# A graph-attention kernel: ScalarE fetches a tile of edges by hand in every 16th pair instead of every 64th, applies z's slope first in its round, and SyncE's queue is reordered

## The chip, the cores and the metric

The kernel runs on one core of one Trainium2 chip. The metric is device time in microseconds (us), taken from runs without the profiler; one further run was profiled. The kernel before takes 3905.68 us (median of three runs, 3905.53 to 3908.12).

## The reference

One layer of a graph network over 12500 nodes with 128 features and 400000 directed edges, each edge with 32 features. The edges arrive sorted by destination; their sources are random.

```
h    = relu(layernorm(x))
n    = layernorm(h) * g1 + b1
x_l, x_r = n @ W_l, n @ W_r                        # 12500 x 128, as 8 heads x 16
e    = edge_attr @ W_e                             # 400000 x 128
m    = leaky_relu(x_l[src] + x_r[dst] + e, 0.2)
alpha = sum over c of m * att                      # one score for each edge and head
a    = softmax of alpha over the edges of one destination (and a loop edge for each node)
h    = h + segment_sum(x_l[src] * a, dst) + bias
out  = x + h + W2 @ gelu(W1 @ layernorm(h))        # written here without its biases
```

What matters here is `x_l[src]`: 400000 rows of 544 bytes (128 features and 8 ones) that lie scattered in a DRAM table, `xl_dram`, and have to be brought into on-chip memory 128 at a time.

## The kernel before, in words

The kernel has three stages. The **node stage** (lines 792 to 879) normalises the nodes and writes `xl_dram` and a part of `xr_dram`, while GpSimd (POOL) already gathers 116 tiles of raw node rows (`raw_gather`, L339), which serve 29 of the later pairs. The **edge stage** (`window_edges`) takes up nearly all the time. The **node groups** (`f_...` steps) finish 25 groups of four tiles of 128 nodes (three in the first and the last) while the edge stage goes on; the last two end it.

The edge stage works in 782 *pairs* of 512 edges, four *tiles* of 128 edges each. A round r of the loop at L1680 writes out, for each engine, one step of each of some ten pairs; every engine then runs its own list in that order, and semaphores alone tie the lists together. The steps of a pair c, with the engine, the round and the line:

- `gather` (POOL, round c-4, L1078): one indirect DMA for each tile of 128 rows, into `xs`, a ring of 12 pairs.
- `combine` (TensorE, round c, L1143 and L1146): turns the four tiles into the PSUM bank `z` and adds the edges' and destinations' part. `apart` (TensorE, round c+2, L1152).
- `slope` (ScalarE, round c+1, L1157): `zs` = 0.2 z. `bend` (VectorE, round c+1, L1162): `m` = max(z, zs).
- `score` (TensorE, round c+2, L1167), `lowest` (VectorE, round c+3, L1173): `rec`.
- `weigh` (ScalarE, round c+3, L1184): `p`, two exponentials. `turn` (TensorE, round c+4, L1192): `pt_ps`.
- `keep_turned` (ScalarE, round c+5, L1197): copies `pt_ps` to `pt`.
- `collect` (TensorE, round c+6, L1206), `own_heads` (VectorE, round c+7, L1215 and L1221).
- `put` (SyncE, round c+8, L1230): stores `rec` to the states in DRAM.

SyncE (SP) also starts the loads of four pairs at once (`windows`, L1104 to L1119), the clearing of states (`clear`, L787), the sums over edge features (`sum_load`, L1248, 98 loads in the first 196 rounds), and the loads and stores of the node groups.

Two ways go around POOL for single tiles. For 35 pairs (every 22nd from 30) SyncE fetches the fourth tile row by row, and for 11 pairs (every 64th from 77) ScalarE does: `hand` (L1037) starts, spread over the 22 or 64 rounds that end six rounds before the pair, 128 DMAs of one 544-byte row each (L1056), whose addresses it reads into registers sixteen at a time (L1010) from `hand_sb`. `gather` then leaves that tile out. One round before the pair, the fetching queue waits until all 128 rows have landed (L1043). `hand_sb` is filled in the node stage: two DMAs (L841) pick the indices out of `src` element by element, and VectorE scales them (L851).

In each round the loop runs `hand` for both ways after all steps on the engines, then `clear`, then `windows`, then `put`. A store carries no order against other stores where rows were fetched in its round (`if fetched`); in the last rounds, where none are, each store waits until the one before has landed.

The steps of the last but one node group stand in the table `soon`, by rounds counted from that group's round, 774: its exponential at +2 (`f_exp`), its square root at +7 (`f_root`), its scaling at +8 (`f_scale`).

Of the kernel before, what the change touches and what calls it, by code (L numbers as in the profile page):

```python
# [13 lines left out]
F32 = mybir.dt.float32  # L14
# [8 lines left out]
P = 128  # L23
# [52 lines left out]
BESIDE_EVERY = 64  # L76
BESIDE_FIRST = 77
BESIDE_LANDED = 3
BESIDE_AT = 64
BIG = 2.0**126  # L80
# [94 lines left out]
def tile_gnn(  # L175
# [112 lines left out]
    def load_consts():  # L288
        for i, v in enumerate((ln2_g, ln2_b, None, b1[0:P], b1[P : 2 * P])):
            if v is not None:  # L290
                nc.sync.dma_start(cols[:, 2 + i : 3 + i], column(v))
        nc.sync.dma_start(att_c, bass.AP(tensor=att.tensor, offset=att.offset, ap=[[1, C], [C, H], [1, 1]]))
        nc.sync.dma_start(we_sb, bass.AP(tensor=w_e.tensor, offset=w_e.offset, ap=[[P, DE], [0, QP], [1, P]]))
        nc.sync.dma_start(weh_sb[WN:P, :], w_e)
        nc.sync.dma_start(w1_sb, w1)
        nc.sync.dma_start(w2_sb, w2.rearrange("(k p) f -> p k f", p=P))
        nc.sync.dma_start(bias_r, row_bcast(bias, P))
        nc.sync.dma_start(b2_r, row_bcast(b2, P))
        nc.sync.dma_start(first_sb, bass.AP(tensor=dst.tensor, offset=dst.offset, ap=[[0, 1], [UP * U, NU // UP]]))
        for i in range(QP):  # L300
            nc.sync.dma_start(
                at_sb[:, BEHIND:, 1 + i],
                bass.AP(tensor=dst.tensor, offset=dst.offset + (UP * i + 1) * U, ap=[[0, 1], [QU * U, NQU]]),
            )

# [504 lines left out]
    with tc.manual_schedule():  # L810
# [15 lines left out]
        for r in range(max(max(len(qs), 9) + LAST + 1, 16 + PARTS, rows_at[-1] + KEPT + 1)):  # L826
# [11 lines left out]
            if r == 14:  # L838
                nc.sync.dma_start(src_sb, src)
                for at, h in ((0, hands), (BESIDE_AT, beside)):  # L840
                    nc.sync.dma_start(  # L841
                        hand_sb[at : at + len(h)],
                        bass.AP(
                            tensor=src.tensor, offset=src.offset + (h[0] + 1) * UP * KU - 1,
                            ap=[[h.step * UP * KU, len(h)], [NCH * K, P]],
                        ),
                    )
            if r == 16:
                for at, h in ((0, hands), (BESIDE_AT, beside)):
                    rows = hand_sb[at : at + len(h)]  # L850
                    nc.vector.tensor_scalar(rows, rows, float(XW * 4), None, op0=OP.mult)  # L851
# [101 lines left out]
def window_edges(  # L953
# [30 lines left out]
    with ExitStack() as es:  # L984
# [52 lines left out]
        def hand(r, w):  # L1037

            w["new"].clear()
            hands, n = w["pairs"], w["sems"]  # L1040
            i, k = divmod(r + HAND_LEAD + hands.step - hands[0], hands.step)
            if k == HAND_LEAD - 1 and 0 < i <= len(hands):
                all_here = w["queue"].wait_ge(w["landed"][(i - 1) % n], ((i - 1) // n + 1) * P * 16)  # L1043
                tc.declare_fence(all_here.ins, group=f"{w['name']}{i - 1}")
# [3 lines left out]
            if k == 0:  # L1048
                d["x"] = once.tile([P, XW], F32, name=f"{w['name']}{i % 2}")
            for e in range(P * k // hands.step, P * (k + 1) // hands.step):  # L1050
                if e % HAND_READ == 0:
                    d["at"] = words(
                        hand_sb[w["at"] + i : w["at"] + i + 1, e : min(e + HAND_READ, P)], (NT * P - 1) * XW * 4,
                        w["engine"],
                    )
                row = w["queue"].dma_start(  # L1056
                    d["x"][e : e + 1, :].bitcast(U8), rows_at(xl_dram, d["at"][e % HAND_READ], 1, XW * 4)
                )
# [166 lines left out]
        def put(c):  # L1225
# [11 lines left out]
            if fetched:  # L1237
# [3 lines left out]
                )  # L1241

# [3 lines left out]
        def sum_load(i):  # L1246
            sums[i] = fin.tile([P, LW], F32, name="ea_s", tag="big", bufs=3)
            nc.sync.dma_start(  # L1248
# [295 lines left out]
        def f_put(d):  # L1544
# [4 lines left out]
            (LATE + 1, own_heads),  # L1549
            (5, keep_turned),  # L1550
# [6 lines left out]
            (1, slope),  # L1557
# [3 lines left out]
        )  # L1561
        late_stages = (
            (-WAHEAD, windows),
            (LATE + PUT, put),
# [115 lines left out]
        with tc.manual_schedule():  # L1680
            for r in range(-AHEAD, max(last_round, groups[-1]["round"] + 18)):
                in_round(r, early, groups[:-2])
                for late, f in stages:
                    c = r - late
                    if 0 <= c < n_pr:
                        f(c)
                for late, f in sum_stages:
# [11 lines left out]
                for w in ways:  # L1699
                    hand(r, w)  # L1700
# [364 lines left out]
```

## Time and profile before

| | us |
|---|---|
| median of three runs | 3905.68 |
| the profiled execution's own time | 3904.92 |
| its span, first to last instruction | 3903.2 |
| POOL's first gather of the edge stage starts | 153.92 |
| POOL's last gather starts | 3854.66 |

A page of the profile gives busy times by engine and the costliest groups of instructions. In a row of a group stand the line, the engine, the operation, the output and inputs by the program's names, the count, then the busy time, the mean of one in ns, and the time that the engine sat idle just before these, with what ended that idle time ("issue": nothing that the profile shows). "ACTq" and "SPq" are the instructions with which ScalarE's and SyncE's sequencers start DMAs or load registers; they are not counted as busy.

### The profile page before, as it was taken

The numbers are of one execution on the slowest core, as the hardware profiler recorded it, in microseconds if no ns is written. First come the engines' busy times: TensorE is split into PE (matmuls) and PEld (weight loads), VectorE is DVE, ScalarE is ACT, GpSimd is POOL, SyncE is SP. The second block draws the span as 40 slices with busy tenths as digits, with TensorE's granted clock in tenths as the row PEclk, the third lists the DMA queues.
The fourth block names the chain that finished last, engine by engine and source line by source line (L and its number), as shares of the span: only waits on it lengthen the run. The fifth ranks groups of instructions, "written<-read, shape, count | busy, mean of one in ns | idle before, by whom it ended". The sixth has DMA issues, their size and how long they took to land.

```text
span 3903.2 us, 70516 instructions
## 1 busy us (share of the span) xinstructions
PE 3414.5 (87%) x18461; PEld 2329.9 (60%) x18463; DVE 2799.8 (72%) x6142; ACT 2177.5 (56%) x4745; POOL 2913.6 (75%) x3092
## 2 busy tenths in 40 slices
PE   3588899889899989998999899999998989898988
PEld 3356566556566666665666666666666666666655
DVE  5577877777776776777777777777777767667665
ACT  6545555555565555555555555655555556456444
POOL 7777777777777777777777777777777777777773
PEclk6799999999999999999999999999999999999999
DMA  8767777777766666665565555555565555555553
GB/s 203 236 163 173 184 184 182 177 185 185 177 135 134 136 131 130 137 132 125 123 131 124 123 126 126 125 123 121 121 125 126 123 123 112 124 122 117 122 119 65
DMA packets 546765, 549.30 MB, mean 141 GB/s; under 512 B 248891, under 2 KB 425372, under 8 KB 545932
## 3 DMA queue, kind: packets, MB, share of 16 engines
q1 hardware_dynamic: 444290, 329.68, 34.3%
q0 software_dynamic: 98528, 214.12, 28.9%
q8 instruction: 150, 2.46, 0.3%
q14 instruction: 261, 2.14, 0.2%
q10 hardware_dynamic: 3536, 0.91, 0.1%
HBM read 482.08 MB, written 62.28 MB: 139 GB/s over the span
## 4 chain that ended last, share of the span: by engine, by line
PE 36%; POOL 24%; DMA 20%; issue 13%; DVE 2%; SPq 1%; ACT 0%; ACTq 0%; POOLq 0%
POOL xs L1078 24%; DMA xs<-xl_dram,src_sb 19%; PE z L1146 8%; PE acc L1206 8%; PE ab L1167 6%; PE pt_ps L1192 4%; PE z L1143 4%; PE ab L1152 2%; PE acc L1525 1%; DMA state<-rec 0%; DVE rec L1173 0%; PE acc L1500 0%; PE pt_ps L759 0%; DMA zw<-xr_dram 0%; PE acc L1328 0%
## 5 line engine op out<-in xcount | busy, mean ns | idle before, releaser
L1078 POOL DMA_INDIRECT xs<-xl_dram,src_sb x2963 | 2798.4, 944 | 904.3 <-issue 783.9
L1184 ACT ACTIVATE p<-ab,rec 128x256 f32<-128x256 f32 x1563 | 656.4, 471 | 923.6 <-DVE rec L1173 909.3
L1215 DVE TENSOR_TENSOR own<-acc,diag 128x272 f32<-128x272 f32 x782 | 342.6, 438 | 821.9 <-PE acc L1206 813.2
L1143 PE MATMUL z<-ident,xs 128*128 128x128 f32 x3079 | 564.7, 283 | 360.6 <-DMA xs<-xl_dram,src_sb 337.9
L1206 PE MATMUL acc<-xs,pt 128*128 128x136 f32 x6158 | 873.7, 286 | 0.0
L1143 PEld LDWEIGHTS z<-ident,xs 128*128 128x128 f32 x3079 | 395.3, 142 | 776.8 <-DMA xs<-xl_dram,src_sb 449.7
L1146 PE MATMUL z<-ea,zw 128*128 128x512 f32 x1564 | 828.0, 612 | 6.5 <-DMA xs<-xl_dram,src_sb 6.5
L1197 ACT COPY pt<-pt_ps 128x512 f32<-128x512 f32 x782 | 456.2, 583 | 643.6 <-PE pt_ps L1192 585.5
L1167 PE MATMUL ab<-m,negrep 128*128 128x512 f32 x1564 | 806.4, 597 | 0.2 <-issue 0.2
L1206 PEld LDWEIGHTS acc<-xs,pt 128*128 128x128 f32 x6158 | 800.7, 197 | 0.0
L1192 PEld LDWEIGHTS pt_ps<-ident,p 128*128 128x128 f32 x3125 | 408.0, 146 | 345.0 <-issue 269.7
L1162 DVE TENSOR_TENSOR m<-z,zs 128x512 f32<-128x512 f32 x782 | 533.6, 682 | 108.1 <-ACT zs L1157 106.2
L1129 DVE TENSOR_SCALAR ea<-dl,wid 96x516 f32<-96x516 bf16 x782 | 575.4, 736 | 8.0 <-DMA dl<-dc_dram 8.0
L1173 DVE TENSOR_REDUCE rec<-ab 128x2 f32<-128x512 f32 x781 | 539.0, 690 | 14.2 <-PE ab L1167 13.7
L1192 PE MATMUL pt_ps<-ident,p 128*128 128x128 f32 x3125 | 490.7, 281 | 0.6 <-ACT p L1184 0.6
L1157 ACT ACTIVATE zs<-z 128x512 f32<-128x512 f32 x782 | 471.8, 603 | 31.0 <-PE z L1146 31.0
L1221 DVE TENSOR_REDUCE rec<-own 128x34 f32<-128x272 f32 x782 | 340.9, 436 | 26.7
L1152 PE MATMUL ab<-ne,farw 128*128 128x512 bf16 (+1 forms) x781 | 306.8, 393 | 24.6 <-ACT p L1184 22.9
L1146 PEld LDWEIGHTS z<-ea,zw 128*128 128x128 f32 x1564 | 253.1, 202 | 7.3 <-issue 6.8
L1167 PEld LDWEIGHTS ab<-m,negrep 128*128 128x128 f32 x1564 | 245.8, 195 | 1.1 <-DMA ea_s<-in_ea_t 0.7
L1152 PEld LDWEIGHTS <-farw 128*128 128x128 bf16 x782 | 78.1, 100 | 211.9 <-issue 102.2
L1184 ACT ACT_TABLE_LOAD x102 | 130.9, 1283 | 1.8
(249 smaller groups left out, 2215.6 us busy)
## 6 DMA issues: line engine op xcount, KB each, us to landing
dl<-dc_dram SPq DMA_DIRECT2D x196, 396.0 KB
hand<-xl_dram SPq DMA_DIRECT2D x4480, 0.5 KB
ea<-in_ea_t SPq DMA_DIRECT2D x196, 256.0 KB
ea_s<-in_ea_t SPq DMA_DIRECT2D x98, 512.0 KB
xs<-xl_dram,src_sb POOLq DMA_INDIRECT x2963
beside<-xl_dram ACTq DMA_DIRECT2D x1408, 0.5 KB
state<-empty SPq DMA_DIRECT2D x98, 144.0 KB
f_st<-state SPq DMA_DIRECT2D x46, 288.0 KB
```

The costliest lines, as they stand in the source:

```text
L1078: nc.gpsimd.indirect_dma_start(out=xs[:, j, :], out_offset=None, in_=xl_dram, in_offset=bass.IndirectOffsetOnAxis(ap=src_sb[:, c * KP + j ...
L1129: nc.vector.tensor_scalar(d["ea"][0:WN].rearrange("p (a b) -> p a b", b=OW), d["dl"][0:WN].rearrange("p (a b) -> p a b", b=OS)[:, :, 0:OW] ...
L1143: nc.tensor.matmul(z[:, j * P : (j + 1) * P], row_of(c, j)[:, 0:P], ident, start=(j == 0), stop=False, is_transpose=True)
L1146: nc.tensor.matmul(z[:, :e], d["zw"], d["ea"][:, :e], start=False, stop=True)
L1152: nc.tensor.matmul(d["ab"][:, :e], d["far"], d["ne"][:, :e], start=True, stop=False)
L1157: nc.scalar.activation(d["zs"][:, :e], d["z"][:, :e], AF.Copy, scale=SLOPE)
L1162: nc.vector.tensor_tensor(d["m"][:, :e], d["z"][:, :e], d["zs"][:, :e], op=OP.max)
L1167: nc.tensor.matmul(d["ab"][:, :e], negrep.rearrange("p n h -> p (n h)"), d["m"][:, :e], start=False, stop=True)
L1173: nc.vector.tensor_reduce(d["rec"][:, :, CX], d["ab"].rearrange("p (u e) -> p u e", e=U), AX.X, OP.min)
L1184: nc.scalar.activation(d["p"][:, us], d["ab"][:, us], AF.Exp, bias=d["rec"][:, i, CX:SH], scale=-1.0)
L1192: nc.tensor.transpose(d["pt_ps"][:, js], d["p"][:, js], ident)
L1206: nc.tensor.matmul(d["acc"][:, i, :], d["pt"][:, j * P : (j + 1) * P], row_of(c, j), start=(j == js[0]), stop=(j == js[-1]),)
```

## The change

1. The distance of the pairs whose fourth tile ScalarE fetches falls from 64 to 16, and the first is pair 29 instead of 77: 47 pairs instead of 11. POOL has 36 indirect DMAs fewer. ScalarE starts 47 x 128 = 6016 row DMAs instead of 1408 and loads registers from `hand_sb` 376 times instead of 88.
2. ScalarE's rows of a round no longer stand together at its end: half follow `keep_turned`, a quarter `weigh`, and a quarter `slope` of the next round. `slope` moves ahead of `keep_turned` and so is first in ScalarE's round.
3. `hand_sb` is no longer filled by DMA: in rounds 24 to 26 of the node stage VectorE copies the wanted columns of `src_sb` as floats, TensorE turns them, VectorE scales them.
4. SyncE's rows are split, half at the start of a round and half after the steps; then comes `put`, then `windows`, then `clear`. After each fourth store the registers for the next four pairs are loaded ahead.
5. The last three stores no longer wait for the landing of the one before (they wait for the last hand-fetched tile instead).
6. `sum_load`'s 98 loads go out on ScalarE's queue instead of SyncE's.
7. In `soon` the steps from `f_exp` on come 1 to 3 rounds earlier: square root at +4, scaling at +5.

```diff
-BESIDE_EVERY = 64
-BESIDE_FIRST = 77
+BESIDE_EVERY = 16
+BESIDE_FIRST = 29
...
+    def hand_columns():
+        nc.vector.memset(hand_f, 0.0)
+        for at, h in ((0, hands), (BESIDE_AT, beside)):
+            first = (h[0] + 1) * UP * KU - 1
+            step = h.step * UP * KU
+            nc.vector.tensor_copy(
+                hand_f[:, at : at + len(h)], src_sb[:, first : first + step * (len(h) - 1) + 1 : step]
+            )
+    def hand_turn():
+        hand_ps["t"] = once_ps.tile([P, GN * P], F32, name="w_ps")
+        nc.tensor.transpose(hand_ps["t"][0 : BESIDE_AT + len(beside), 0:P], hand_f, ident)
+    def hand_bytes():
+        nc.vector.tensor_scalar(
+            hand_sb, hand_ps["t"][0 : BESIDE_AT + len(beside), 0:P], float(XW * 4), None, op0=OP.mult
+        )
...
-                for at, h in ((0, hands), (BESIDE_AT, beside)):
-                    nc.sync.dma_start(
-                        hand_sb[at : at + len(h)],
...
-        def hand(r, w):
+        def hand(r, w, share=(0, 1), behind=0):
...
-            for e in range(P * k // hands.step, P * (k + 1) // hands.step):
+            first, last = P * k // hands.step, P * (k + 1) // hands.step
+            for e in range(*(first + int((last - first) * x) for x in share)):
...
+            free = bool(fetched) or c > hands[-1]
+            if free and not fetched:
+                nc.sync.wait_ge(ways[0]["landed"][(len(hands) - 1) % LANDED], ((len(hands) - 1) // LANDED + 1) * P * 16)
...
-            if fetched:
+            if free:
...
+            if c % QP == 0 and c + QP < n_pr:
+                ats(c // QP + BEHIND + 1)
...
-            nc.sync.dma_start(
+            nc.scalar.dma_start(
                 sums[i],
...
             (LATE + 1, own_heads),
+            (1, slope),
             (5, keep_turned),
...
-            (1, slope),
...
+        beside_at = {keep_turned: ((0, 0.5),), weigh: ((0.5, 0.75),), slope: ((0.75, 1), 1)}
         late_stages = (
+            (LATE + PUT, put),
             (-WAHEAD, windows),
-            (LATE + PUT, put),
...
-            (2, f_exp),
-            (3, f_den),
-            (4, f_out),
-            (5, f_h),
-            (6, f_stats),
-            (7, f_root),
-            (8, f_scale),
-            (8, f_rest),
+            (1, f_exp),
+            (2, f_den),
+            (2, f_out),
+            (3, f_h),
+            (3, f_stats),
+            (4, f_root),
+            (5, f_scale),
+            (5, f_rest),
...
+                hand(r, ways[0], (0, 0.5))
                 in_round(r, early, groups[:-2])
...
+                    if f in beside_at:
+                        hand(r, ways[1], *beside_at[f])
...
-                for w in ways:
-                    hand(r, w)
+                hand(r, ways[0], (0.5, 1))
+                for late, f in late_stages:
+                    c = r - late
+                    if 0 <= c < n_pr:
+                        f(c)
...
-                for late, f in late_stages:
-                    c = r - late
-                    if 0 <= c < n_pr:
-                        f(c)
```

Three places show what the engines' lists become. A row is a line of the program, the operation, output and input, the shape, and how many such stand in a row; `beside` is ScalarE's hand-fetched tile, `hand` SyncE's.

ScalarE in the middle of the edge stage, kernel before, one round (with one step for later nodes' `xr` rows, L669, such as stands in some rounds):

```order
L1197 COPY pt<-pt_ps 128x512
L1157 ACTIVATE zs<-z 128x512
L1184 ACTIVATE p<-ab,rec 128x256 x2
L669 ACTIVATE xr_14292<-pt_ps,cols 128x512
L1056 DMA beside_11620<-xl_dram 1x544 x2
```

The same engine in the changed kernel, one round:

```order
L1176 ACTIVATE zs<-z 128x512
L1075 DMA beside_24432<-xl_dram 1x544 x2
L1216 COPY pt<-pt_ps 128x512
L1026 TENSOR_LOAD hand_sb
L1075 DMA beside_24432<-xl_dram 1x544 x4
L1203 ACTIVATE p<-ab,rec 128x256 x2
L1075 DMA beside_24432<-xl_dram 1x544 x2
```

`zs` now comes ahead of `pt`; eight row DMAs a round stand in three places where two stood in one, and in every second round, as here, a register load stands between `pt` and `p`.

SyncE around the loads of four pairs, before:

```order
L787 DMA state<-empty 128x2x144
L1010 TENSOR_LOAD at_sb
L1104 DMA ea<-in_ea_t 32x4x512
L1109 DMA dl_1711<-dc_dram 96x2112
L1114 DMA du_1714<-du_dram 64x1x512
L1119 DMA zw_1705<-xr_dram 96x512
L1230 DMA state<-rec 96x2x72
L1056 DMA hand_23106<-xl_dram 1x544 x6
```

and in the changed kernel:

```order
L1252 DMA state<-rec 96x2x72
L1026 TENSOR_LOAD at_sb
L1123 DMA ea<-in_ea_t 32x4x512
L1128 DMA dl_1713<-dc_dram 96x2112
L1133 DMA du_1716<-du_dram 64x1x512
L1138 DMA zw_1708<-xr_dram 96x512
L809 DMA state<-empty 128x2x144
L1075 DMA hand_30322<-xl_dram 1x544 x6
```

The store has moved from behind the four loads to ahead of them, and the clearing from ahead of everything to the end.

ScalarE in the last rounds, before (`zs` of 128x128 is the last pair's, whose single tile is all that is left):

```order
L1184 ACTIVATE p<-ab,rec 128x256 x2
L1449 ACT_TABLE_LOAD
L1449 ACTIVATE f_rstd<-f_rstd 128x4
L1197 COPY pt<-pt_ps 128x512
L1157 ACTIVATE zs<-z 128x128
L1184 ACT_TABLE_LOAD
L1184 ACTIVATE p<-ab,rec 128x256 x2
L1463 ACTIVATE f_hn<-h_sb,f_nmr,f_rstd 128x128 x4
```

and in the changed kernel the same steps of the node group, from the square root to the next round's `p`:

```order
L1473 ACT_TABLE_LOAD
L1473 ACTIVATE f_rstd<-f_rstd 128x4
L1176 ACTIVATE zs<-z 128x512
L1216 COPY pt<-pt_ps 128x512
L1203 ACT_TABLE_LOAD
L1203 ACTIVATE p<-ab,rec 128x256 x2
L1487 ACTIVATE f_hn<-h_sb,f_nmr,f_rstd 128x128 x4
```

The `zs` between them is now a full one of 512 columns: the node group's steps stand three rounds ahead of the last pair's `zs`, where before they stood around it.

More of the change, by code (lines that the diff above doesn't have):

```diff
@@ L839, in tile_gnn @@
                 nc.sync.dma_start(src_sb, src)
-                for at, h in ((0, hands), (BESIDE_AT, beside)):
-                    nc.sync.dma_start(
-                        hand_sb[at : at + len(h)],
[L843 to L851, printed above, removed]
+            if r == HAND_ROUND:
+                hand_columns()
+            if r == HAND_ROUND + 1:
+                hand_turn()
+            if r == HAND_ROUND + 2:
+                hand_bytes()
             if r == 10:
@@ L1236, in put @@
             tc.add_to_no_dep_group("states", store.ins)
-            if fetched:
+            if free:
                 tc.declare_no_dep(
```

15 lines of the change are left out of this document (10 added, 5 removed).

## The prediction

> **What bounds the kernel now.** I read the page's busy times first, then the groups of GpSimd (POOL) for the stretch from 200 to 3800 us, then the waits of each engine, then the end in order of time. By busy time TensorE leads:
>
> ```profile
> span 3903.2 us, 70516 instructions
> PE 3414.5 (87%) x18461; PEld 2329.9 (60%) x18463; DVE 2799.8 (72%) x6142; ACT 2177.5 (56%) x4745; POOL 2913.6 (75%) x3092
> ```
>
> That order misleads. The group of POOL's gathers in that stretch, the timeline around its first gather of the edge stage, and its last two gathers:
>
> ```profile
> L1078 POOL DMA_INDIRECT xs<-xl_dram,src_sb x2882 | 2722.0, 944 | 878.9 <-issue 761.4 <-DMA xs<-xl_dram,src_sb 39.9 <-PE pt_ps L1192 24.1
> ...
> 151.88 0.94 POOL L339 DMA_INDIRECT raw<-in_x,src_raw  x1 [0.31 <-issue]
> 153.92 0.94 POOL L1078 DMA_INDIRECT xs<-xl_dram,src_sb  x1 [1.10 <-issue]
> ...
> 3853.41 0.94 POOL L1078 DMA_INDIRECT xs<-xl_dram,src_sb  x1 [0.30 <-issue]
> 3854.66 0.94 POOL L1078 DMA_INDIRECT xs<-xl_dram,src_sb  x1 [0.30 <-issue]
> ```
>
> Busy and idle together are 2722.0 + 878.9 = 3600.9 us, the whole stretch, and per gather 3600.9 / 2882 = 1.249 us. From the first start to the last, 3854.66 - 153.92 = 3700.7 us pass for 2962 steps: again 1.249 us each. So the 0.30 us before each gather is the price of issuing one, not a wait, and POOL never stops for anyone. The idle time put down to other engines is the same 0.30 us under another name.
>
> Who waits for POOL? TensorE's longest wait, and the two of ScalarE (ACT) that matter:
>
> ```profile
> PE z L1143 <- DMA xs<-xl_dram,src_sb: 337.9, 338, 12.7
> ACT p L1184 <- DVE rec L1173: 909.3, 612, 5.9
> ACT pt L1197 <- PE pt_ps L1192: 585.5, 464, 7.4
> ```
>
> TensorE stands 337.9 us, waiting for rows that POOL has fetched too late. The kernel is POOL's list of gathers from 153.9 to 3855.6 us (the last one's end), and then a tail of 47.6 us to the span's end.
>
> **The change: POOL's part.** 47 - 11 = 36 gathers leave POOL's list. At 1.249 us that is 45.0 us. What is late next is TensorE, and it has 337.9 us in hand against the 45.0 that it must win. Whether it wins them depends on ScalarE.
>
> **ScalarE's part.** The price of a row, a register load and a sum load, from the answers for the tiles and lines, and one place where rows are issued today:
>
> ```profile
> L1010 ACTq TENSOR_LOAD <-hand_sb x88: 1188/1199/1785, 196.5 to 3488.8; - x88
> L1248 SPq DMA_DIRECT2D ea_s<-in_ea_t x98: 366/442/1352, 163.1 to 1063.4; - x98
> ...
> 2002.85 0.47 ACT L1184 ACTIVATE p<-ab,rec 128x256 f32<-128x256 f32 x1 [1.74 <-DVE rec L1173]
> 2002.92 0.23 ACTq L1056 DMA_DIRECT2D beside<-xl_dram  x1
> 2003.23 0.47 ACT L1184 ACTIVATE p<-ab,rec 128x256 f32<-128x256 f32 x1
> 2003.24 0.23 ACTq L1056 DMA_DIRECT2D beside<-xl_dram  x1
> 2003.59 0.59 ACT L1197 COPY pt<-pt_ps 128x512 f32<-128x512 f32 x1
> ```
>
> One row follows another after 0.32 us. In all that is 6016 x 0.32 = 1925 us, and with 376 register loads of 1.2 us (451) and 98 sum loads of 0.44 us (43) 2419 us of issuing, where today it is 1408 x 0.32 + 88 x 1.2 = 556. The upper bound is that none of it runs beside the engine's own work. The row of sums over the windows from 200 us to the end gives that work:
>
> ```profile
> sum 3703.00, PE 3323.13 PEld 2260.06 DVE 2683.95 ACT 2055.24 POOL 2763.51; mean PE 830.78 PEld 565.01 DVE 670.99 ACT 513.81 POOL 690.88
> ```
>
> 2055 + 2419 = 4474 us, against 3703 - 45 = 3658 us that POOL leaves: ScalarE would be the bound by far. The lower bound is that all of it hides: nothing. The rows above are nearest: both row DMAs go out while the two `p` run, the second `p` starts 0.38 us after the first as elsewhere, and `pt` follows 0.36 us after that. The queue issues DMAs while the engine works off instructions it already holds. To stay below POOL, 816 of the 2419 us, **34%**, must hide. The new places suit that. Per round (3700.7 / 782 = 4.73 us) ScalarE waits 909.3 / 782 = 1.16 us ahead of `p` and 585.5 / 782 = 0.75 us ahead of `pt`. Ahead of `p` now stand four rows (1.28 us), and in every second round a register load (1.2 us), partly beside `pt` (0.58 us); two rows (0.64 us) stand ahead of `pt`, beside `zs` (0.60 us), and two beside the `p`. In rounds with a register load `p` comes about 0.7 us later than it would; its reader, `turn`, stands in TensorE's next round, so it hides. I take zero, near the lower bound.
>
> The hardest stretch is where ScalarE has node groups and table loads besides; the fullest ten rounds that I found:
>
> ```profile
> 1127.00:1174.00 47.00, 43.18 (x239) 29.14 (x238) 35.30 (x82) 36.95 (x75) 35.72 (x38) 1.00 0.62 127
> ```
>
> ACT is busy 36.95 of 47 us (fourth column). Ten rounds' issuing (80 rows and five loads) is 31.6 us, so here (36.95 + 31.6 - 47) / 31.6 = 68% must hide, or ScalarE falls behind for a few rounds. The ring of 12 pairs in `xs` lets POOL go on meanwhile.
>
> **Moves at one price.** `zs` ahead of `pt` costs nothing: `z` is finished earlier in TensorE's round than `pt_ps`, and VectorE waits 106.2 us for `zs` in all:
>
> ```profile
> DVE m L1162 <- ACT zs L1157: 106.2, 96, 2.8
> ```
>
> Its gain is hidden behind POOL too. The wait for the 128 landed rows stands in ScalarE's queue ahead of four fetches and `p`, but six rounds (28 us) after the last of the rows, so it finds them there: zero; if not, TensorE, which needs the tile a round later, would wait as well. SyncE's new order delays the loads for four pairs by one store and its wait; they run four rounds ahead: zero. The sum loads may make ScalarE wait for earlier transfers. On SyncE no such wait of L1248 stands among the longer ones; I take zero, and 98 x 0.4 us, one more issue each, as the upper end, hidden like the rest.
>
> **The node stage.** SyncE loses an issue of 13 us and VectorE a wait of 11.3:
>
> ```profile
> 76.68 13.21 SPq L841 DMA_DIRECT2D hand_sb<-in_src  x2
> DVE hand_sb L851 <- DMA hand_sb<-in_src: 11.3, 2, 9.7
> L851 DVE TENSOR_SCALAR hand_sb<-hand_sb x2: 219/296/372, 91.2 to 92.9; 35x128 int32<-35x128 int32 x1, 11x128 int32<-11x128 int32 x1
> ```
>
> But POOL's 116 raw gathers go on to 151.88 us whatever the others do; only the step from the last raw gather to the first of the edge stage, 2.04 us instead of 1.25, could shrink: 0.8 us at most. The new copies on VectorE are small (nearest row 0.2 to 0.4 us, four of them: under 2 us), and less than the wait that goes. I take -0.4, between -0.8 and +2.
>
> **The tail.** ScalarE's timeline and the chain of waits near the end:
>
> ```profile
> 3863.66 0.84 ACT L1184 ACTIVATE p<-ab,rec 128x256 f32<-128x256 f32 x2 [2.16 <-DVE rec L1173]
> 3864.52 1.28 ACT L1449 ACT_TABLE_LOAD   x1
> 3865.81 0.20 ACT L1449 ACTIVATE f_rstd<-f_rstd 128x4 f32<-128x4 f32 x1
> ...
> 3866.69 1.28 ACT L1184 ACT_TABLE_LOAD   x1
> ...
> 3868.71 1.64 ACT L1463 ACTIVATE f_hn<-h_sb,f_nmr,f_rstd 128x128 f32<-128x128 f32 x4
> ...
> 3875.46 0.14 DVE rec L1221
> 3875.60 1.48 DMA state<-rec
> ...
> 3877.21 1.48 DMA state<-rec
> ...
> 3878.81 1.40 DMA state<-rec
> 3880.23 2.86 DMA f_st<-state
> ```
>
> The two table loads, the root and the four `f_hn`, 1.28 + 0.20 + 1.28 + 1.64 = 4.4 us, stand on the path to the last pairs' `p`. Moved three rounds up, they stand where TensorE still waits for gathers; late next is VectorE, so I take 3.5 of the 4.4. Three stores then land one after the other. Without that wait the last leaves when its `rec` is there, about 3876.5 instead of 3878.8 us: 2.3. Together -5.8; between 0 (the moved steps crowd the rounds before) and -7.
>
> **Sum.** 3904.9 (the profiled execution's own time) - 45.0 - 0.4 - 5.8 = 3853.7. The median of the runs stands 0.8 above that execution, 0.02%, so I forecast **3854**; with the ends of the terms 3845 to 3866.
>
> A rule that speaks against the change: the Trainium skill's "DMA: Bandwidth & Descriptors" (section "Issuing engines are not separate DMA queues") says that DMAs started on several engines share the same 16 DMA engines, so that spreading them saves only the issuing time, "usually small relative to the DMA itself". By that rule nearly nothing would be won. Here the trace speaks against it: issuing is what binds, 1.249 us without a pause.
>
> **Rivals.**
>
> *ScalarE becomes the bound* (slower). Place: its queue from pair 7 to 760. For it: 2419 us of issuing in a queue with about 1650 us to spare, and the engine must hold `pt` and `p` while rows are issued. Against it: the hiding shown at 2002.85. It decides under 32% hidden (4474 - 3703 = 771 of 2419: slower than before). At a quarter hidden: 2055 + 0.75 x 2419 = 3869 us for the stage, 166 more than 3703: 4071 us.
>
> *ScalarE is late only in the full stretches.* There 68% must hide. At half hidden, ten such rounds lose 36.95 + 15.8 - 47 = 5.7 us, less what the ring lends. With 23 node groups and 1 us lost to each: 3854 + 23 = 3877.
>
> *The DMA engines are what the gathers wait for* (no change). The same bytes move, so the time would stay at 3905. For it, TensorE's wait names a DMA; against it, the rate at which POOL issues, and the DMA engines' share:
>
> ```profile
> 200.00:3800.00 3600.00, 3238.71 (x17624) 2203.54 (x17624) 2624.82 (x5414) 2011.43 (x4166) 2721.31 (x2882) 0.97 0.64 139
> ```
>
> They are busy 0.64 of the time (last column but one).
>
> **How the numbers follow.** Forecast 0.77, late stretches 0.10, ScalarE the bound 0.08, no change 0.05. The range takes the forecast's own ends and most of the late stretches: 3845 to 3885; what lies above it is 0.16 or so. A measurement of this kernel can tell about 0.2% (7.8 us) from no change. Faster by more, below 3898: 0.77 + 0.09 = 0.86; within 0.2%: 0.05; slower: 0.09, with 0.01 for a lateness that eats all.
>
> **What would show it.** In the changed kernel's profile POOL's gathers should number 2927, still 1.249 us apart, the last one starting near 3854.7 - 45.4 = 3809.3 us. TensorE's wait for `xs` should fall to about 290 us and not vanish. ScalarE's waits ahead of `p` and `pt` should shrink to well under their 909 and 585 us, without TensorE waiting for `p` or `pt` instead. The tail behind the last gather should be about 42 us. I am wrong if steps between POOL's gathers grow beyond 1.25 us, waiting for `collect`: then ScalarE has taken over, and POOL's 36 gathers were not what was worth saving.

## The result and the profile after

The changed kernel takes 3898.3 us (median of 20 runs, 3889.1 to 3906.8), the kernel before 3905.6 us (median of 20, 3902.4 to 3908.1). The ratio is 0.9982, with a 95% interval of 0.9975 to 0.9988: a gain of 0.2% where 1.3% was forecast. The profiled execution is the shortest of the 20, 3889.1 us. Its page begins so, and its first group is GpSimd's (POOL's) gathers:

```profile
span 3887.3 us, 80725 instructions
PE 3414.2 (88%) x18462; PEld 2332.2 (60%) x18464; DVE 2799.9 (72%) x6144; ACT 2177.5 (56%) x4745; POOL 2878.6 (74%) x3056
...
L1097 POOL DMA_INDIRECT xs<-xl_dram,src_sb x2927 | 2763.6, 944 | 929.4 <-issue 746.3
```

The gathers number 2927, as they should. The first and the last of them in its timeline:

```profile
152.68 0.95 POOL L1097 DMA_INDIRECT xs<-xl_dram,src_sb  x1 [0.30 <-issue]
...
3844.36 0.95 POOL L1097 DMA_INDIRECT xs<-xl_dram,src_sb  x1 [0.30 <-PE pt_ps L1211]
```

From one start to the other 3691.7 us pass. 2926 steps of 1.249 us are 3654.6, so **POOL stood still for 37.1 us** in between (the same sum gives 1.2 us for the kernel before). The tail behind the last start is 3887.3 - 3844.4 = 42.9 us; it was 48.5. So the list gave 45.0 us, the start 1.2, the tail 5.6, and the stall took 35.9 back: 15.9 us of span.

Where POOL stood still is read by counting gathers per stretch. The rows of one stretch, first of the kernel before, then of the changed one (the fifth count is POOL's):

```profile
400.00:1400.00 1000.00, 897.51 (x4860) 607.40 (x4861) 770.63 (x1550) 567.40 (x1210) 756.06 (x801) 0.98 0.72 166
```

```profile
400.00:1400.00 1000.00, 876.00 (x4690) 590.93 (x4689) 743.32 (x1498) 547.85 (x1175) 728.42 (x772) 0.96 0.67 162
1400.00:3800.00 2400.00, 2193.29 (x12056) 1500.90 (x12055) 1736.53 (x3635) 1363.75 (x2779) 1813.90 (x1922) 0.98 0.57 127
```

772 gathers instead of 801 are 29 x 1.249 = 36 us: the whole stall lies between 400 and 1400 us. Behind 1400 us, 1922 gathers in 2400 us are 1.249 us each again. The waits of the changed kernel over the whole span that answer to those shown of before:

```profile
ACT p L1203 <- DVE rec L1192: 664.9, 347, 5.8
DVE m L1181 <- ACT zs L1176: 306.0, 215, 7.3
PE z L1162 <- DMA xs<-xl_dram,src_sb: 188.4, 202, 4.0
PEld pt_ps L1211 <- ACT pt L1216: 56.6, 39, 4.3
POOL xs L1097 <- PE acc L1225: 56.0, 70, 5.6
ACT pt L1216 <- PE pt_ps L1211: 49.1, 51, 3.9
```

POOL waits for `collect` (`acc`), up to 5.6 us at a time: the ring of 12 pairs is full. TensorE waits 188 us for gathers where 290 were forecast, and VectorE waits three times as long for `zs`. TensorE also waits 56.6 us for `pt`, a wait that the prediction hoped not to see. ScalarE was my first suspect.

One more difference stands in SyncE's waits from 400 to 1400 us. Of the kernel before, and of the changed one, the wait of the stores (`put`) for the landing of a `clear`:

```profile
SPq L1230 <- DMA state<-empty: 4.4, 7, 1.0
```

```profile
SPq L1252 <- DMA state<-empty: 136.6, 52, 4.7
```

### The profile page after: what moved, and what is told of

It is laid out like the page before. It is cut to its first block, busy times and chain, and to the rows that moved or that the text cites. A ratio compares the mean times of both kernels' runs of the same rounds, so it can differ in the third digit from the quotient of the medians.

```text
span 3887.3 us, 80725 instructions
## 1 busy us (share of the span) xinstructions
PE 3414.2 (88%) x18462; PEld 2332.2 (60%) x18464; DVE 2799.9 (72%) x6144; ACT 2177.5 (56%) x4745; POOL 2878.6 (74%) x3056
## 4 chain that ended last, share of the span: by engine, by line
PE 39%; DMA 19%; POOL 14%; issue 9%; DVE 6%; ACTq 5%; ACT 3%; SPq 2%; POOLq 0%; DVEq 0%
DMA xs<-xl_dram,src_sb 13%; POOL xs L1097 13%; PE acc L1225 9%; PE z L1165 8%; PE ab L1186 7%; PE pt_ps L1211 5%; PE z L1162 4%; ACTq L1075 3%; PE ab L1171 2%; DMA du<-du_dram 1%; DMA zw<-xr_dram 1%; DVE ea L1148 1%; DVE rec L1192 1%; DVE m L1181 1%; DMA state<-rec 1%
## 5 line engine op out<-in xcount | busy, mean ns | idle before, releaser
L1097 POOL DMA_INDIRECT xs<-xl_dram,src_sb x2927 | 2763.6, 944 | 929.4 <-issue 746.3
L1225 PEld LDWEIGHTS acc<-xs,pt 128*128 128x128 f32 x6086 | 792.0, 197 | 0.8 <-DVE f_wt L1389 0.8
L1181 DVE TENSOR_TENSOR m<-z,zs 128x512 f32<-128x512 f32 x782 | 534.2, 683 | 311.3 <-ACT zs L1176 306.0
L1162 PE MATMUL z<-ident,xs 128*128 128x128 f32 x3043 | 527.1, 281 | 233.4 <-DMA xs<-xl_dram,src_sb 188.4
```

Of the source, the lines that this page charges most:

```text
L1097: nc.gpsimd.indirect_dma_start(out=xs[:, j, :], out_offset=None, in_=xl_dram, in_offset=bass.IndirectOffsetOnAxis(ap=src_sb[:, c * KP + j ...
L1162: nc.tensor.matmul(z[:, j * P : (j + 1) * P], row_of(c, j)[:, 0:P], ident, start=(j == 0), stop=False, is_transpose=True)
L1181: nc.vector.tensor_tensor(d["m"][:, :e], d["z"][:, :e], d["zs"][:, :e], op=OP.max)
L1225: nc.tensor.matmul(d["acc"][:, i, :], d["pt"][:, j * P : (j + 1) * P], row_of(c, j), start=(j == js[0]), stop=(j == js[-1]),)
```

## The experiments

Eighteen runs. Twelve of them (names with e, p, r, s) came out in sessions in which the kernel before takes 5047 to 5055 us, called the 5050 us sessions below; POOL is not the bound there, so ratios are told, but sizes do not carry over. Six (n, q) came out where it takes 3904 or 3905 us. The expectations speak of different chips, which the record does not show: it gives chips 8 and 9 for the six, and 0 and 9 for the twelve, so number 9 stands on both sides. "Stall" is what is left of the time between POOL's first and last start after steps of 1.249 us, as worked out above.

| kernel | us | ratio to before (95%) | gathers | stall, us |
|---|---|---|---|---|
| before | 3905.6 | 1 | 2963 | 1.2 |
| changed | 3898.3 | 0.9982 (0.9975 to 0.9988) | 2927 | 37.1 |
| n1, sum loads back on SyncE | 3914.0 | 1.0027 (1.0016 to 1.0038) | 2927 | 60.3 |
| n2, ScalarE fetches from pair 237 on | 3910.5 | 1.0020 (1.0009 to 1.0032) | 2940 | 40.8 |
| n3, ScalarE fetches every 64th | 3937.3 | 1.0087 (1.0055 to 1.0120) | 2963 | 43.6 |
| n4, before with every 16th alone | 3933.2 | 1.0077 (1.0048 to 1.0106) | 2927 | 39.2 |
| q1, SyncE's old order | 3879.4 | 0.9937 (0.9920 to 0.9953) | 2927 | 22.3 |
| q2, store, clear, loads | 3858.7 | 0.9882 (0.9865 to 0.9898) | 2927 | 8.1 |

### Whose queue is late: ScalarE's or SyncE's

Theory S: the sum loads, now in ScalarE's queue, wait there for other transfers. Theory R: ScalarE has too many rows to issue where node groups and raw pairs crowd. Theory O: SyncE's new order is late. Four kernels are to tell them apart (n1 to n4). Three of them were run in a 5050 us session too (e1, e3, e4), with e2 in the place of n2.

```diff
 n1, e1 (from the changed kernel)
-            nc.scalar.dma_start(
+            nc.sync.dma_start(
                 sums[i],
 n2
-BESIDE_FIRST = 29
+BESIDE_FIRST = 237
 n3, e3
-BESIDE_EVERY = 16
+BESIDE_EVERY = 64
-BESIDE_FIRST = 29
+BESIDE_FIRST = 77
 n4, e4 (from the kernel before)
-BESIDE_EVERY = 64
+BESIDE_EVERY = 16
-BESIDE_FIRST = 77
+BESIDE_FIRST = 29
 e2 (from the kernel before)
-            nc.sync.dma_start(
+            nc.scalar.dma_start(
                 sums[i],
```

Expected of n1: 

> The changed kernel with the 98 sum loads issued by SyncE again, as before the change; all else of the change stays. The profile of the changed kernel shows GpSimd stalled for 37.5 us beyond its 1.249 us steps, 36 us of it between 400 and 1400 us. Theory S (the sum loads wait in ScalarE's queue for other transfers and hold up zs, pt and p behind them): the stall falls below 8 us, and the time to about 3862 us. Theory R (ScalarE has too much issuing of rows in the crowded stretch, whatever the sum loads do): the stall stays between 25 and 45 us, and the time between 3890 and 3905 us. Theory O (SyncE's new order brings the four-pair loads late): the stall grows, since SyncE has 98 more transfers in that order, and the time is above 3900 us.

Expected of n2: 

> The changed kernel with ScalarE's fetching begun at pair 237 in place of 29, every 16th pair from there: 13 fetches fewer, all of them from the crowded stretch, so GpSimd has 13 gathers more, 16.2 us. The sum loads stay on ScalarE. Theory R: the stall falls below 8 us, and the time is 3898 - 30 + 16 = about 3880 us. Theory S: the waits of the sum loads stay, so does most of the stall (above 20 us), and the time is 3900 to 3915 us. Theory O: as S.

Expected of n3: 

> The changed kernel with ScalarE fetching in every 64th pair from pair 77 as before the change; the sum loads on ScalarE, SyncE's new order and the turned indices stay. GpSimd issues 36 gathers more than in the changed kernel, as many as before. Theory R: no stall above 5 us, and the time is that of before less what the start and the end gain (7 us): about 3898 us. Theory S: 20 us of stall or more, and the time is 3915 to 3935 us. Theory O: stall of 20 us or more, with late four-pair loads ahead of it.

Expected of n4: 

> The kernel before with nothing changed but that ScalarE fetches in every 16th pair from pair 29: the sum loads stay on SyncE, and SyncE's order and slope's place are the old ones. GpSimd issues 36 gathers fewer, 45.0 us. Theory S: no stall above 8 us, and the time is about 3862 us. Theory R: a stall of 25 us or more between 400 and 1400 us, more if slope's place matters, and the time is 3885 us or more. Theory O: no stall, about 3862 us.

**S falls** as the main cause. With the sum loads back on SyncE (n1) the stall grows to 60.3 us and the time by 15.7: 3914.0. But n1 has a new lateness of its own: VectorE waits there for the sum loads themselves, from 400 to 1400 us, where in the changed kernel it waits 0.2 us for them in all.

```profile
DVE part L1278 <- DMA ea_s<-in_ea_t: 88.2, 29, 4.4
```

So n1 does not show what the stall would be if nothing waited for sum loads. **R falls.** Where ScalarE fetches nothing before pair 237 (n2), or only in every 64th pair (n3), the stall stays, 40.8 and 43.6 us. It need not be the same stall, since in these two SyncE also waits for ScalarE's sum loads (27.2 and 10.7 us in that stretch), which it does not in the changed kernel; the clean proof against R is q2 below, with all 47 fetches and 8.1 us of stall. In n2 and n3 the lateness is open to see. The waits of n3 between 400 and 1400 us:

```profile
DVE ea L1148 <- DMA dl<-dc_dram: 78.3, 23, 5.5
POOL xs L1097 <- PE acc L1225: 51.0, 29, 5.5
...
PE z L1165 <- DMA zw<-xr_dram: 19.7, 11, 4.1
```

and SyncE's there:

```profile
SPq L1252 <- DMA state<-empty: 135.1, 49, 5.4
```

VectorE and TensorE wait for `dl` and `zw`, two of the four-pair loads that were to come four rounds ahead; in the kernel before neither wait is there. That is what O says.

n4 shows two more things. Its time is 28 us above before: 45.0 us won on POOL's list, 38 lost to the stall, 33.6 lost at the start and 1 in the tail. A raw gather in its node stage, the first gather of its edge stage, the wait of VectorE in the node stage, and VectorE's longest wait:

```profile
128.22 0.94 POOL L339 DMA_INDIRECT raw<-in_x,lead  x1 [31.66 <-DMA raw_dram<-raw]
...
187.53 0.94 POOL L1078 DMA_INDIRECT xs<-xl_dram,src_sb  x1 [3.91 <-issue]
...
DVE hand_sb L851 <- DMA hand_sb<-in_src: 44.2, 2, 36.0
...
DVE m L1162 <- ACT zs L1157: 793.8, 460, 6.1
```

Picking 47 + 35 rows of indices out by DMA lets VectorE wait 44.2 us (11.3 with 11 + 35). In SyncE's queue the next store of `xl_dram` is then issued for 36.7 us, and POOL's raw gathers stand for 31.66 us, waiting for a store behind it. So the change's third edit, the indices turned by TensorE, is what keeps the start where it was. And with rows in one lump and `slope` late, VectorE waits 793.8 us for `zs`: here ScalarE does hold things up. The changed kernel, with the rows spread and `slope` early, has 306.0; which of the two edits is needed was not run apart.

In a 5050 us session:

Expected of e1: 

> The changed kernel with the 98 sum loads back on SyncE's queue, all else as changed. Theory S (the sum loads' waits for earlier transfers stand in ScalarE's in-order queue and hold up zs, pt and p): the 37 us that POOL lost between 400 and 1400 us come back, about 3854 us. Theory R (ScalarE simply has too much issuing in the stretches where node groups, raw pairs and table loads crowd): next to nothing comes back, 3890 to 3898 us. Theory O (SyncE's new order brings the loads of four pairs too late): 3890 to 3898 us as well.

Expected of e2: 

> The kernel before with nothing changed but the 98 sum loads, which go out on ScalarE's queue. Theory S: the same waits appear there, but with two rows a round instead of eight ScalarE has some 2 us a round to spare; POOL loses little, 3905 to 3915 us, and waits ahead of ScalarE's instructions for transfers of SyncE show in the profile. Theories R and O: 3905 us and no such waits.

Expected of e3: 

> The changed kernel with ScalarE's fetches back at every 64th pair (from 77), all else as changed, sum loads on ScalarE too. Theory S: 3905 less about 7 for tail and node stage, plus what the waits cost a less loaded ScalarE: 3898 to 3908 us. Theory R: 3898 us, POOL without a stop. Theory O: 3898 plus the lateness of the loads, 3910 to 3935 us.

Expected of e4: 

> The kernel before with ScalarE's fetches at every 16th pair (from 29) and nothing else: eight rows at the end of each round, pt ahead of zs, sum loads on SyncE. Theory S: 45 us less than before, about 3860 us. Theory R: most of the 45 us is lost again, 3890 to 3905 us. Theory O: 3860 us.

Measured: e1 5086.8 us, ratio 1.0073 (1.0043 to 1.0103); e2 5041.3, 0.9977 (0.9955 to 0.9999); e3 4998.8, 0.9880 (0.9838 to 0.9922); e4 5137.6, 1.0159 (1.0117 to 1.0201). Every number expected is missed: the kernel before itself takes 5047 us there, and POOL waits 493 to 606 us for `collect` in these four. Where POOL is not the bound, fetching in every 16th pair is a loss (e4 against before 90 us), and the rest of the change a gain (e3).

### Which part of SyncE's order

Theory C: the clear, now issued behind four loads, lands late, and the store that comes next in SyncE's queue waits for it. Theory F: the loads are late because a store stands ahead of them. Theory N: neither. SyncE's timeline in the changed kernel shows one such wait:

```profile
801.16 0.36 SPq L1252 DMA_DIRECT2D state<-rec  x1
802.88 0.34 SPq L1123 DMA_DIRECT2D ea<-in_ea_t  x1
...
804.48 0.34 SPq L1138 DMA_DIRECT2D zw<-xr_dram  x1
804.87 0.42 SPq L809 DMA_DIRECT2D state<-empty  x1
...
807.05 0.92 SPq L1075 DMA_DIRECT2D hand<-xl_dram  x3
809.95 0.36 SPq L1252 DMA_DIRECT2D state<-rec  x1
```

The last of the rows is out at 807.97, the store at 809.95: SyncE stands for 2 us, until the clear of 804.87 has landed. 136.6 us in 52 such waits are 2.6 us each, once in four rounds (some 19 us). The last clear is issued at 1934.9 us. The waits alone do not make a stall: from 1400 to 1950 us the stores wait 49.9 us more, and POOL runs in steps of 1.249 us; the stall lies nearly all between 600 and 1400 us. What else must come together there is not shown; the sum loads (the last at 1098 us) are one candidate.

```diff
 q1, p1 (from the changed kernel): clear, loads, store
+                (the clear, unchanged)
                 for late, f in late_stages:
...
-                (the clear)
         late_stages = (
-            (LATE + PUT, put),
             (-WAHEAD, windows),
+            (LATE + PUT, put),
 q2, p2: store, clear, loads
-                for late, f in late_stages:
+                for late, f in late_stages[:1]:
...
                 (the clear, unchanged)
+                for late, f in late_stages[1:]:
+                    c = r - late
+                    if 0 <= c < n_pr:
+                        f(c)
 p3: the clear two rounds later, behind the first rows of its round
-                hand(r, ways[0], (0, 0.5))
+                hand(r, ways[0], (0, 0.2))
+                t, off = divmod(r - 2, CLEAR)
...
+                hand(r, ways[0], (0.2, 0.5))
 p4, r1, s1 (from the kernel before): store, loads, clear
         late_stages = (
+            (LATE + PUT, put),
             (-WAHEAD, windows),
-            (LATE + PUT, put),
...
                 for late, f in late_stages:
...
+                (the clear, moved behind)
```

The p runs came out in a 5050 us session.

Expected of p1: 

> The changed kernel with SyncE's order at the end of a round as it was before the change: the clear, the four-pair loads, the store. All else of the change stays. Three theories are left for GpSimd's 37 us of stall. Theory C: the store that comes next after a clear waits until the clear has landed; in the new order the clear is issued behind four loads and lands late, so SyncE, some 80% occupied in that stretch, falls behind (117.6 us of such waits between 400 and 1200 us). Theory F: putting the store ahead of the loads by itself makes the loads late, since they queue behind its wait for rec. Theory N: it is something else of the change (the node groups' steps drawn together, slope's place). C and F: the stall falls below 8 us and the time to about 3862 us. N: the stall stays above 25 us and the time near 3898 us.

Expected of p2: 

> The changed kernel with the clear between the store and the loads: store, clear, loads; the next store comes a round later, as in the changed kernel. Theory C: the clear lands early again, the stores' waits for it fall from 117.6 us below 30 us between 400 and 1200 us, GpSimd's stall falls below 8 us, and the time is about 3862 us. Theory F: the loads still come behind the store, so the stall stays above 25 us, and the time is near 3898 us. Theory N: as F.

Expected of p3: 

> The changed kernel with the clear moved half a group away from the loads: it is issued two rounds later, behind the first of that round's fetched rows, half a round ahead of that round's store. Store and loads keep the new order. Theory C: the clear no longer has the loads' transfers ahead of it, so the stores' waits for it fall below 60 us between 400 and 1200 us (it is nearer to its store than in the other order, some 2 us), GpSimd's stall falls below 15 us, and the time is 3860 to 3875 us. Theories F and N: the stall stays above 25 us, and the time is near 3898 us.

Expected of p4: 

> The kernel before with nothing changed but SyncE's order at the end of a round: store, loads, clear as in the changed kernel. The sum loads stay on SyncE, and ScalarE fetches in every 64th pair. Theory C: the stores wait for the clears (over 80 us between 400 and 1200 us), the four-pair loads come late, GpSimd stalls for 30 to 65 us, and the time is 3935 to 3970 us. Theory F: the same. Theory N: no stall above 5 us, and the time is that of before, 3904 us.

Measured: p1 5025.2 us, ratio 0.9960 (0.9933 to 0.9986); p2 5020.5, 0.9935 (0.9909 to 0.9961); p3 5038.5, 0.9985 (0.9961 to 1.0010); p4 5082.6, 1.0060 (1.0039 to 1.0082). The new order alone makes the kernel before slower (p4), as C and F both have it. The changed kernel itself was not run in that session, so p1 to p3 have nothing to be held against, and the sizes do not carry over. p1 and p2 once more, where the kernel before takes 3905.1 us:

Expected of q1: 

> The same edit once more, for the same reason: the changed kernel with SyncE's old order, clear, loads, store. It gave 0.996 of the kernel before where that took 5050 us. Theories C and F: GpSimd's stall falls below 8 us, and the time is about 3862 us. Theory N: the stall stays above 25 us, and the time near 3898 us.

Expected of q2: 

> The same edit once more, wanted on a chip on which the kernel before takes 3904 us: the changed kernel with the clear between the store and the loads. Where the kernel before took 5050 us, this edit gave 0.9935 of it, and the stores waited for clears for 0 us between 400 and 1400 us. Theory C (the clear behind the loads holds up the next store, and SyncE falls behind): GpSimd's stall falls from 37 us below 8 us, and the time is about 3862 us. Theory F (the loads come late because a store is ahead of them): the stall stays above 25 us, and the time near 3898 us. Theory N (something else of the change): as F.

q2 takes **3858.7 us** (3857.7 to 3861.7): moving the clear by four instructions is worth 39.6 us. Its first and last gather, its row of the stretch, and its stores' waits there:

```profile
153.24 0.95 POOL L1097 DMA_INDIRECT xs<-xl_dram,src_sb  x1 [0.30 <-issue]
...
3815.95 0.94 POOL L1097 DMA_INDIRECT xs<-xl_dram,src_sb  x1 [0.31 <-PE z L1162]
...
400.00:1400.00 1000.00, 894.14 (x4899) 604.93 (x4898) 770.04 (x1548) 572.85 (x1218) 751.32 (x797) 0.98 0.76 167
...
SPq L1252 <- DMA state<-empty: 32.4, 25, 2.8
```

797 gathers in the stretch, and 32.4 us of waits instead of 136.6. F and N fall: the loads still stand behind a store, and nothing else differs from the changed kernel. C holds, with one miss: q1 should have come out the same, and takes 3879.4 us with a stall of 22.3. Its stores wait three quarters as long as the changed kernel's:

```profile
SPq L1252 <- DMA state<-empty: 106.4, 50, 5.3
```

In q1 the clear comes first, but the store follows in the same round, behind four loads; in q2 a round and its rows lie between. The kernel before has q1's order and only 4.4 us of these waits. What differs is the load of the next pairs' registers: before, it stands between the clear and the four loads, and the change moves it behind a store. A clear and the store that waits for it, in the kernel before and in q1 (the register load is not a row of this view; it fills the time from 801.62 to 803.16):

```profile
801.15 0.43 SPq L787 DMA_DIRECT2D state<-empty  x1
803.27 0.34 SPq L1104 DMA_DIRECT2D ea<-in_ea_t  x1
...
804.87 0.33 SPq L1119 DMA_DIRECT2D zw<-xr_dram  x1
805.39 0.35 SPq L1230 DMA_DIRECT2D state<-rec  x1
```

```profile
813.32 0.42 SPq L809 DMA_DIRECT2D state<-empty  x1
813.84 0.42 SPq L1123 DMA_DIRECT2D ea<-in_ea_t  x1
...
815.52 0.37 SPq L1138 DMA_DIRECT2D zw<-xr_dram  x1
817.65 0.35 SPq L1252 DMA_DIRECT2D state<-rec  x1
```

The medians over that stretch, counted from the clear's start, say the same. SyncE is through with what stands between after 4.05 us in the kernel before, and the store starts at 4.25. In q1 these are 2.59 and 4.72, in the changed kernel 3.48 and 5.99, in q2 5.52 and 6.30. Where nearly every store waits, the second number tells when the clear has landed: 4.7 us after its start in q1, 6.0 in the changed kernel, where four loads go ahead of it. What costs is the part of that time for which SyncE has nothing else to issue before the store. n4, which has the register load in its old place, comes to its store after 4.05 us and has 18.3 us of these waits. No run moved the register load alone, so this reading of q1 is argued from the traces, not tested.

How the lateness reaches TensorE differs. In n2 and n3 the loads themselves are waited for. In the changed kernel VectorE waits 2.8 us in all for `dl` in that stretch. There the chain of waits from 800 us on goes through ScalarE:

```profile
801.16 3.92 DMA state<-rec
805.11 0.37 ACTq L1272
...
805.58 0.04 ACT zs L1176
```

A sum load (L1272) stands at the head of ScalarE's queue until SyncE's store of 801.16 has landed, and `zs` behind it. The two have no data in common; in the trace both count the same completion semaphore, number 117. How much of the 37 us came this way is not shown, but it was hardly the most: from 400 to 1400 us ScalarE's waits that end with a landing sum to 105.4 us in the changed kernel and still to 86.9 in q2, whose stall is 8.1.

### What the parts are worth then

```diff
 r2, s2 (from q2)
-BESIDE_EVERY = 16
+BESIDE_EVERY = 64
-BESIDE_FIRST = 29
+BESIDE_FIRST = 77
```

Expected of r1: 

> The kernel before with nothing changed but SyncE's order at the end of a round: store, loads, clear. The sum loads stay on SyncE, ScalarE fetches in every 64th pair, slope stays behind lowest. (The same edit gave 1.006 of the kernel before where that took 5050 us.) Theory C, by what the runs showed of it (store, clear, loads in the changed kernel gave 3858.7 us, store, loads, clear 3898 us): the stores wait for clears for 100 to 140 us between 400 and 1400 us instead of 4.4, GpSimd stalls for 30 to 65 us, and the time is 3935 to 3970 us. Theory N' (the new order hurts only together with the sum loads on ScalarE): no stall above 8 us, and the time is 3904 us.

Expected of r2: 

> The kernel with store, clear, loads (3858.7 us), but ScalarE fetches in every 64th pair from pair 77 as before the change: GpSimd issues 36 gathers more. If GpSimd's issuing is the bound of that kernel all the way, the time is 3858.7 + 36 x 1.249 = 3903.7 us, with a stall below 9 us, so the rest of the change is worth next to nothing beside the fetching. If the fetching on ScalarE costs something that the stall of 8 us hides, it is 3896 us.

Expected of s1: 

> Once more, wanted on a chip on which the kernel before takes 3904 us: the kernel before with nothing changed but SyncE's order at the end of a round, store, loads, clear. Theory C: the stores wait for clears for 100 to 140 us between 400 and 1400 us instead of 4.4, GpSimd stalls for 30 to 65 us, and the time is 3935 to 3970 us. Theory N' (the new order hurts only together with the sum loads on ScalarE): no stall above 8 us, and the time is 3904 us.

Expected of s2: 

> Once more, for the same reason: the kernel with store, clear, loads, but ScalarE fetches in every 64th pair from pair 77. If GpSimd's issuing is the bound of the kernel with store, clear, loads all the way: 3858.7 + 36 x 1.249 = 3903.7 us, with a stall below 9 us. If the fetching on ScalarE costs something that its stall of 8 us hides: 3896 us.

All four came out in the 5050 us sessions: r1 5075.2 us, 1.0052 (1.0028 to 1.0076), s1 5074.0, 1.0055 (1.0023 to 1.0088); r2 4969.3, 0.9833 (0.9784 to 0.9882), s2 4969.4, 0.9845 (0.9825 to 0.9865). The new order alone is slower there for the third time. r2 and s2 are some 51 us below p2, from which they differ in the fetching alone: a loss there. Where POOL is the bound, the new order was not measured alone; n3, which has the new order and all the rest but the fetching, is 33.7 us above the 3903.5 of the kernel before in its session. What the fetching is worth there stands between n3 and the changed kernel, which have like stalls (43.6 and 37.1 us): 3937.3 - 3898.3 = 39.0 us by the medians (of two runs for n3), 53.4 by the profiled spans, around the list's 45.0.

## Why the prediction was wrong, point by point

- **The step that failed** is "SyncE's new order delays the loads for four pairs by one store and its wait; they run four rounds ahead: zero." It priced the loads and not the clear, which the order shown with the change puts behind them. The next store waits for its landing: 136.6 us in 52 waits where there were 4.4. What stands behind such a store in SyncE's queue, rows and loads, goes out up to 4.7 us later. q2, with the clear four instructions earlier, has 32.4 us of these waits and 8.1 of stall. The step should have held about +36 us, the stall of the profiled execution over that of before; by the medians the clear's place is worth 39.6 us (q2 against the changed kernel). That the clear's place is the cause is shown; by which of its followers the lateness comes to TensorE stays open.
- **POOL's list**: right. 36 gathers fewer at 1.249 us; q2's span is 3903.2 - 45.0 - 0.7 (start) - 4.9 (tail) + 6.9 (stall of 8.1 instead of 1.2) = 3859.5, with the stall as what is left over.
- **ScalarE's issuing at zero**: right within the 6.9 us of stall that q2 has left, and only with the edits that go with it: n4 has the fetching without them and loses 38 us to stalls. The rival "ScalarE late only in the full stretches" named a place inside the right stretch (1127 to 1174 us), but a loss of 23 us spread over 23 node groups, where 36 fell between 400 and 1400 us, and the wrong queue: n2 has no rows of ScalarE's before pair 237 and stalls all the same.
- **The sum loads at zero**: the edit was right. Back on SyncE they cost 15.7 us more (n1). That they wait in ScalarE's queue was named, and is so; what that costs is open.
- **The node stage**: -1.2 us, -0.4 forecast. That is beyond the -0.8 given as the most, since the raw gathers too ended 0.45 us earlier. They do not go on "whatever the others do": with 47 tiles and the old way they stop for a store of SyncE's, and the start is 33.6 us later (n4).
- **The tail**: -5.6 us, -5.8 forecast; the root's table load now stands where POOL still gathers:

```profile
3842.23 1.28 ACT L1473 ACT_TABLE_LOAD   x1
...
3843.52 0.20 ACT L1473 ACTIVATE f_rstd<-f_rstd 128x4 f32<-128x4 f32 x1
...
3844.36 0.95 POOL L1097 DMA_INDIRECT xs<-xl_dram,src_sb  x1 [0.30 <-PE pt_ps L1211]
```

- **The sign to look for** was named: steps between gathers above 1.25 us, waiting for `collect`. The reason given there, that ScalarE has then taken over, was wrong: POOL's gathers were worth saving, as q2 shows.

One thing stays open on size: the profiled execution is 15.9 us below the one of before, the medians differ by 7.3. The changed kernel's runs spread over 17.7 us and q2's over 4.0, so the stall probably differs from run to run; no trace of a longer run was taken.

## What to carry to other kernels

When a change reorders a queue that is nearly full (in the kernel before, SyncE's loads, stores and register instructions take 78% of the time from 400 to 1400 us), follow each transfer that is moved to the next instruction in that queue that waits for its landing, not only to those who read what it brings: here a clear that nobody needs for several rounds held up the store behind it. Give such a transfer its place by how long the queue has something else to issue behind it. And when a stall follows a change of many parts, undo one part at a time before believing the longest wait: the wait for ScalarE's `zs` had grown threefold, and the cause stood in SyncE's queue.

## What the runs showed of the hardware that was not expected

- The same kernel took 3905 us in some sessions and 5047 to 5055 us in others, with a granted clock of 0.96 and 0.88. Some of SyncE's own instructions took far longer there. The register moves ahead of its rows (min, median, max in ns), in the kernel before where it takes 3905 us and in s1:

```profile
L1056 SPq MOVE hand<-xl_dram x4480: 29/29/38, 169.9 to 3807.3; - x195
```

```profile
L1056 SPq MOVE hand<-xl_dram x4480: 2/29/1441, 215.0 to 4989.9; - x195
```

  A move that takes 29 ns at the median takes up to 1441 ns there, while ScalarE's moves (L1056 too) take 38 ns at most in both. POOL in s1 waits 533.5 us for `collect` (`POOL xs L1078 <- PE acc L1206`) and 363.3 us for something that the profile calls remote. What slows these sessions is not settled, nor whether it is the chip.
- Two queues can be tied together by a completion semaphore: a load on ScalarE's queue stood until an unrelated store of SyncE's had landed, 3.9 us after that store was issued.
- Picking single indices out of DRAM for 82 tiles instead of 46 made VectorE wait 44.2 us instead of 11.3, and SyncE's next store took 36.7 us to issue, where it took 1.0.
